# Layer 0's router gates, range count and weight means: one piece a tile, and a matmul three steps later

## The chip, the cores and the metric

The kernel runs on one core of a Trainium2 chip. The metric is device time in microseconds (us) of one launch. The engines are TensorE (PE; its weight loads are shown apart as PEld), VectorE (DVE), ScalarE (ACT), GpSimd (POOL), and SyncE (SP), which issues most DMAs here. Each engine works through its own queue of instructions; they meet at semaphores.

## The reference

Two layers of a metaformer on an image batch of 2 x 256 channels x 56 x 56. Each layer has a spatial mixer and a mixture of experts (MoE) over the 6272 pixels taken as tokens.

```python
# layer 0
x = x + window_attention(_ln_c(x))          # 7x7 windows, 8 heads of 32
t = tokens(x)
t = t + moe0(_ln_t(t))                      # 8 experts, top 2
# layer 1
x = x + ternary_conv_block(_ln_c(x))        # two 3x3 convolutions
t = tokens(x)
t = t + moe1(_ln_t(t))

def moe0(tokens):                           # D = 256, hidden 256
    probs = softmax(tokens @ router_w.T)
    rw, re = top_k(probs, 2);  rw = rw / max(rw.sum(-1), 1e-12)
    out = tokens
    for e in range(8):
        out = out + combine[:, e] * (gelu(tokens @ w1[e]) @ w2[e])

def ternary_weight(w):                      # of each of layer 1's two convolutions
    tw = w - mean(w)
    lo, hi = min(tw) + span / 3, max(tw) - span / 3
    return where(tw < lo, -1, where(tw > hi, 1, 0))
```

What the change touches is the gates of `moe0` (`rw` above), a check that no softmax sum left its range, and the `mean(w)` of the two ternary weights.

## The kernel before, in words

**Layer 0's attention** runs strip by strip (14 strips of 8 x 56 pixels). Each finished strip is normalised, routed and written, row by row of its chosen experts, into a DRAM table `xs` by indirect DMAs of POOL (L891). The largest logits and all logits are kept (`most`, `lgs`), so that the gates can be computed at once for all tokens by `gates0` (L906 to L925): DVE subtractions, two ACT exponentials (L915, L916), then DVE sums, reciprocals and products.

**Layer 0's experts** (`experts_in_order`, L1058) run over 56 tiles of 256 rows, each with one expert's weights. For each tile j the order of the instructions on SP, PE, ACT and DVE is written out by hand (`manual_schedule`):

- SP: `fetch_rows(j + 4)` (L1091) reads rows of `xs`; their place comes from a plan (`where`), a small table in SBUF that SP reads into a register. `fetch_weights(j + 3)` (L1102) reads 641 KB of expert weights.
- `turn(j + 2)`: PE transposes (L1112) into one PSUM buffer `pt`, ACT copies it out as `ut` (L1116), DVE computes destinations (L1119).
- `first(j + 1)`: 8 matmuls (L1144), two ACT gelus (L1151).
- `second(j)`: 8 matmuls (L1163) into one of two `py` buffers; DVE adds the bias into `y` (L1173). POOL scatters `y` into the DRAM table `ys` (L1175). The weight buffer (one of four) is free for `fetch_weights(j + 4)` after this DVE instruction.
- `beside(j)`: other work goes here, at the end of the tile, behind the tile's instructions in every queue.

Tiles 0 to 26 follow an early plan, made when 10 of the 14 strips were routed. The rest needs a second plan (`tiles0(1)`, L931 to L1045): a PE matmul that sums counts (L947), then some 30 small DVE instructions, up to `where` (L1036) and `held` (L1045).

`beside(j)` does the following. While late strips are still being routed, it advances them (`push`). Once none is left, which is in tile 21, it calls `routed_all`, all of it in that one tile: the second plan, the gates, the range count `unfit` on DVE (L1700 to L1703), the matmul `pf` that sums it over the partitions (L1705), and `flag` (L1706). Then it closes the attention's pools, opens the big buffer `x_all` and clears the convolution's borders with POOL memsets (L1722 to L1725). From the next tile on, `beside` takes four steps per tile of the generator `prepare`, which makes the two ternary weights.

**A ternary weight** (`ternary`, L1273) is loaded into `x_all` in pieces of 1024 columns (L1286) and goes through nine parts of 512 columns: DVE maximum (L1293) and minimum (L1295), ACT sum (L1298). Then DVE folds the parts (L1300, L1301), POOL takes the maximum over the partitions (`ext`, L1303), PE sums over the partitions with a matrix of ones (`psum_w`, L1305), and DVE computes the mean (L1307) and thresholds (from L1312, which reads `ext`). A second pass over the nine parts writes -1, 0 and 1 (L1329 to L1333), and last come the copies that the convolutions read (ACT L1340 for the second weight; L1345, L1346, L1826 and DVE L1352 for the first). A step ends at each `yield`: before, 53 steps for the first weight and 47 for the second.

**After the experts** layer 1 reads `ys` back strip by strip (L1215), adds, normalises, convolves, and runs its own MoE. The change leaves these stages as they are; they begin when the last rows of `ys` have landed.

Of the kernel before, what the change touches and what calls it, by code (L numbers as in the profile page):

```python
# [632 lines left out]
def metaformer(ctx: ExitStack, tc: tile.TileContext, a: dict, out: bass.AP, flag):  # L633
# [620 lines left out]
    def finish(steps):  # L1254

        while True:
            try:
                next(steps)
            except StopIteration as end:
                return end.value  # L1260
# [12 lines left out]
    def ternary(name, sums, ps_pool, tag, tp, at):  # L1273

        size = KC * TAPS * C
        wide = NTT * C  # L1280
        raw = x_all.rearrange("p s c -> p (s c)")[:, at * wide : at * wide + size]
        parts = [(n, raw[:, n : n + PART]) for n in range(0, size, PART)]

        def load(i):
            n = min(wide, size - i * wide)
            nc.sync.dma_start(raw[:, i * wide : i * wide + n], a[name + "_flat"][:, i * wide : i * wide + n])  # L1286

        st3 = tp.tile([P, 3, len(parts)], F32, tag="st3", name="st3")
        load(0)
        for i, (n, part) in enumerate(parts):  # L1290
            if n % wide == 0 and n + wide < size:
                load(n // wide + 1)
            nc.vector.tensor_reduce(st3[:, 0, i : i + 1], part, AX.X, ALU.max)  # L1293
            yield
            nc.vector.tensor_reduce(st3[:, 1, i : i + 1], part, AX.X, ALU.min, negate=True)  # L1295
            yield
            low = tp.tile([P, PART], F32, tag="low", name="low", bufs=1)
            nc.scalar.activation(low, part, AF.Copy, accum_out=st3[:, 2, i : i + 1])  # L1298
        st = tp.tile([P, 3], F32, tag="st", name="st")
        nc.vector.tensor_reduce(st[:, 0:2], st3[:, 0:2, :], AX.X, ALU.max)  # L1300
        nc.vector.tensor_reduce(st[:, 2:3], st3[:, 2, :], AX.X, ALU.add)  # L1301
        ext = tp.tile([P, 2], F32, tag="ext", name="ext")
        nc.gpsimd.partition_all_reduce(ext, st[:, 0:2], P, bass_isa.ReduceOp.max)  # L1303
        pt = ps_pool.tile([P, 1], F32, tag=tag, name="psum_w", bufs=3)
        nc.tensor.matmul(pt, ones, st[:, 2:3], start=True, stop=True)  # L1305
        mean = tp.tile([P, 1], F32, tag="w_mean", name="w_mean")
        nc.vector.tensor_scalar_mul(mean, pt, 1.0 / NW)  # L1307

        hi = tp.tile([P, 1], F32, tag="w_hi", name="w_hi")
        lo = tp.tile([P, 1], F32, tag="w_lo", name="w_lo")  # L1310
        third = tp.tile([P, 1], F32, tag="w_third", name="w_third")
        nc.vector.tensor_tensor(hi, ext[:, 0:1], mean, ALU.subtract)  # L1312
        nc.vector.scalar_tensor_tensor(
            lo, ext[:, 1:2], -1.0, mean, ALU.mult, ALU.subtract
        )
        span = tp.tile([P, 1], F32, tag="w_span", name="w_span")
        rest = tp.tile([P, 1], F32, tag="w_rest", name="w_rest")
        nc.vector.tensor_tensor(span, hi, lo, ALU.subtract)
        nc.vector.tensor_scalar_mul(third, span, 1.0 / 3.0)


        nc.vector.scalar_tensor_tensor(rest, third, -2.0, span, ALU.mult, ALU.add)
        nc.vector.tensor_tensor(rest, rest, third, ALU.subtract)
        nc.vector.scalar_tensor_tensor(third, rest, 1.0 / 3.0, third, ALU.mult, ALU.add)
        nc.vector.tensor_tensor(lo, lo, third, ALU.add)
        nc.vector.tensor_tensor(hi, hi, third, ALU.subtract)
        for n, part in parts:
            low = tp.tile([P, PART], F32, tag="low", name="low", bufs=1)
            nc.vector.tensor_scalar(low, part, mean, lo, ALU.subtract, ALU.is_lt)  # L1329
            yield  # L1330
            nc.vector.tensor_scalar(part, part, mean, hi, ALU.subtract, ALU.is_gt)
            yield
            nc.vector.tensor_tensor(part, part, low, ALU.subtract)  # L1333
            yield
        g = raw.rearrange("p (k y c) -> p k y c", k=KC, y=3)
        middle = g[:, :, 1, C : 2 * C]
        nc.vector.tensor_scalar_mul(middle, middle, 2.0)
        if sums.shape[2] == 3:
            for k in range(KC):
                nc.scalar.copy(sums[:, k], g[:, k])  # L1340
                yield
            return
        for k in range(KC):
            up, middle, down = (g[:, k, y, :] for y in range(3))
            nc.scalar.copy(sums[:, k, 0, :], up)  # L1345
            nc.scalar.copy(sums[:, k, 3, :], down)  # L1346
            nc.vector.tensor_tensor(up, up, down, ALU.add)
            yield
            nc.vector.tensor_scalar_mul(middle, middle, 0.5)
            yield  # L1350
            for c, op in ((1, ALU.add), (2, ALU.subtract)):
                nc.vector.scalar_tensor_tensor(sums[:, k, c, :], up, 0.5, middle, ALU.mult, op)  # L1352
                yield
# [4 lines left out]
    with ExitStack() as st:  # L1358
# [72 lines left out]
        norm0, settle0, tiles0, _, gates0, wgt0, counted0, sent0 = routing(0, aw, tp, ps)  # L1431
# [202 lines left out]
        plans0, taken = [], []  # L1634
# [54 lines left out]
        X, XT, pad, sums = {}, {}, {}, []  # L1689
# [4 lines left out]
        def routed_all():  # L1694

            nonlocal x_all
            plans0.append(tiles0(1, *taken))
            finish(gates0())
            unfit = aw.tile([TT, 1], F32, tag="unfit", name="unfit")
            nc.vector.tensor_scalar(fits, fits, float(len(STRIPS)), None, ALU.is_lt)  # L1700
            nc.vector.tensor_reduce(unfit, fits, AX.X, ALU.add)
            unfit_b = aw.tile([TT, 1], BF16, tag="unfit_b", name="unfit_b")
            nc.vector.tensor_copy(unfit_b, unfit)  # L1703
            pf = ps.tile([P, 1], F32, tag="aux", name="pf")
            nc.tensor.matmul(pf, all_w, unfit_b, start=True, stop=True)  # L1705
            nc.vector.tensor_scalar_min(flag, pf[0:1, :], 1.0)  # L1706
            st.close()

            xpool = mid_x.enter_context(tc.tile_pool(name="x", bufs=1, reuse_waits="tile"))


            x_all = xpool.tile([P, len(STRIPS), NTT * C], F32, tag="x", name="x")
            for i, (b, s) in enumerate(STRIPS):
                XT[b, s] = x_all[:, i].rearrange("p (t c) -> p t c", c=C)
                X[b, s] = x_all[:, i, : KC * NT].rearrange("p (k n) -> p k n", n=NT)

            for b in reversed(range(B)):
                cp = pads[b].enter_context(
                    tc.tile_pool(name=f"pads{b}", bufs=1, reuse_waits="tile")
                )  # L1720
                t = cp.tile([P, HC, KC, WC], F32, tag=f"pad{b}", name=f"pad{b}")
                nc.gpsimd.memset(t[:, 0:1], 0.0)  # L1722
                nc.gpsimd.memset(t[:, HC - 1 : HC], 0.0)
                nc.gpsimd.memset(t[:, 1 : HC - 1, :, 0:1], 0.0)
                nc.gpsimd.memset(t[:, 1 : HC - 1, :, WC - 1 : WC], 0.0)  # L1725
                pad[b] = t
            mid.enter_context(wq_held)
            wqp = wq_held.enter_context(tc.tile_pool(name="wq", bufs=1, reuse_waits="tile"))

            some = x_all[:, len(STRIPS) - 3 :].rearrange("p s c -> p (s c)").bitcast(BF16)  # L1730
            sums.append(some.rearrange("p (k n c) -> p k n c", k=KC, n=COMPS))
            sums.append(wqp.tile([P, KC, 3, 3 * C], BF16, tag="sums", name="sums"))

        def prepare():
            for i in range(2):
                yield from ternary(f"L1_conv_w{i + 1}", sums[i], ps0, "ph", tp0, 5 * i)

        steps = prepare()

        def beside(j):  # L1740
            push()
            if j == NTILE - 2:

                for i in range(X_FIRST):
                    nc.sync.dma_start(XT[STRIPS[i]][:TT], x_mid[i])
            if j == EARLY[0] - ROWS_AHEAD - 1:
                while under_way:
                    push()
            if len(plans0) > 1:
                for _ in range(4):  # L1750
                    next(steps, None)
            elif not under_way:
                routed_all()

        experts(0, C, plans0, ys[0], wp0, tp0, ps0, beside)
        for _ in steps:
            pass
        tiles_on.close()

    with mid:  # L1760
# [336 lines left out]
        with ExitStack() as both:  # L2097
# [50 lines left out]
            norm, settle, tiles, planning, gates, wgt1, _, sent = routing(1, wp, tp, ps)  # L2148
# [241 lines left out]
```

## Time and profile before

| | |
|---|---|
| Median of 3 runs | 1796.24 us (1790.43 to 1796.35) |
| The profiled execution's own time | 1794.06 us |
| Its span in the profile | 1792.3 us |
| Mean granted TensorE clock | 0.883 |
| PE busy | 1535.1 us (86%) |
| DVE busy | 970.1 us (54%) |
| ACT busy | 698.9 us (39%) |
| POOL busy | 672.7 us (38%) |

The profile is one execution. Times in it count from the start of its span. A group's idle time is that of its engine just before the instruction, with what ended it. A PE at 86% is not idle 14% evenly: the share is an average over stages that have different limits, so a change inside layer 0's experts is read from the stretch of some 200 us in which they run.

### The profile page before, as it was taken

The numbers are of one execution on the slowest core, as the hardware profiler recorded it, in microseconds if no ns is written. First come the engines' busy times: TensorE is split into PE (matmuls) and PEld (weight loads), VectorE is DVE, ScalarE is ACT, GpSimd is POOL, SyncE is SP. The second block draws the span as 40 slices with busy tenths as digits, with TensorE's granted clock in tenths as the row PEclk, the third lists the DMA queues.
The fourth block names the chain that finished last, engine by engine and source line by source line (L and its number), as shares of the span: only waits on it lengthen the run. The fifth ranks groups of instructions, "written<-read, shape, count | busy, mean of one in ns | idle before, by whom it ended". The sixth has DMA issues, their size and how long they took to land. (4 is left out here: it accounts for less than half of the span.)

```text
span 1792.3 us, 25968 instructions
## 1 busy us (share of the span) xinstructions
PE 1535.1 (86%) x8613; PEld 1202.6 (67%) x8613; DVE 970.1 (54%) x2697; ACT 698.9 (39%) x1358; POOL 672.7 (38%) x772
## 2 busy tenths in 40 slices
PE   5999998999878868894799979957579999999953
PEld 3555565556557747774688768846468888888842
DVE  4456666465635336864799888778633112111146
ACT  2544343443323324642444362234333334334312
POOL 2112445344343653543243323427715553222210
PEclk9999998999879888997799989955569999999975
DMA  7122334122266766976654000024447778888868
GB/s 233 41 64 85 107 92 131 58 75 62 77 192 213 246 205 226 321 250 201 175 155 126 8 0 1 11 62 128 125 159 268 267 244 287 288 289 286 288 178 287
DMA packets 91887, 291.78 MB, mean 163 GB/s; under 512 B 20487, under 2 KB 35803, under 8 KB 80416
## 3 DMA queue, kind: packets, MB, share of 16 engines
q1 hardware_dynamic: 66736, 231.79, 41.4%
q0 software_dynamic: 21200, 51.82, 8.1%
q10 hardware_dynamic: 3808, 6.42, 1.1%
q8 instruction: 70, 1.15, 0.3%
q14 instruction: 73, 0.60, 0.1%
HBM read 218.51 MB, written 74.20 MB: 163 GB/s over the span
## 5 line engine op out<-in xcount | busy, mean ns | idle before, releaser
L1144 PE MATMUL ph<-ut,w 128*128 128x256 f32 (+1 forms) x1472 | 315.1, 366 | 6.6 <-DMA w<-in_L_experts 6.5
L1173 DVE TENSOR_TENSOR y<-py,w 128x512 f32<-128x512 f32 (+1 forms) x120 | 76.8, 640 | 440.8 <-PE py L1163 362.3
L1163 PE MATMUL py<-w,h 128*128 128x256 f32 x1288 | 303.7, 384 | 7.1 <-issue 7.1
L1144 PEld LDWEIGHTS ph<-ut,w 128*128 128x128 f32 x1472 | 254.8, 197 | 36.0 <-DMA w<-in_L_experts 6.3
L1163 PEld LDWEIGHTS py<-w,h 128*128 128x128 f32 x1288 | 247.3, 194 | 42.5 <-issue 8.5
L891 POOL DMA_INDIRECT xs<-u,pos x224 | 219.0, 978 | 125.1 <-issue 53.6
L1175 POOL DMA_INDIRECT ys<-y,dest x136 | 137.1, 1008 | 246.3 <-DVE dest L1119 110.1
L1151 ACT ACTIVATE h<-ph,w 128x256 f32<-128x256 f32 (+1 forms) x368 | 162.9, 447 | 132.5 <-PE ph L1144 89.0
L1522 ACT ACTIVATE ex<-sc 112x476 f32<-112x476 f32 (+3 forms) x224 | 116.8, 572 | 176.3 <-PE sc L1512 165.4
L1116 ACT COPY ut<-pt 128x512 f32<-128x512 f32 (+1 forms) x120 | 65.2, 543 | 268.8 <-PE pt L1112 231.0
L1842 PE MATMUL pc<-lo,wq 128*128 128x448 f32 x336 | 132.2, 395 | 6.7 <-DVE lo L1817 6.6
L1842 PE MATMUL pc<-hi,wq 128*128 128x448 f32 x336 | 131.4, 393 | 2.2 <-DVE x L1866 2.0
L1532 PE MATMUL av<-ex,vals 112*64 112x238 f32 (+3 forms) x896 | 127.0, 406 | 5.3 <-DVE acc L1542 3.3
L1175 POOL DMA_INDIRECT ys<-y,to x81 | 82.3, 1016 | 130.9 <-DVE dest L1119 78.3
L1542 DVE TENSOR_TENSOR acc<-av,acc 128x238 f32<-128x238 f32 (+3 forms) x224 | 87.0, 406 | 75.1 <-PE av L1532 67.5
L1234 DVE SCALAR_TENSOR_TENSOR x<-got,wgt,x 112x256 f32<-112x256 f32 x216 | 102.6, 544 | 31.9 <-DMA got<-ys 31.5
L1985 PE MATMUL pc<-hi,wq 128*128 128x448 f32 (+1 forms) x288 | 103.4, 369 | 16.8 <-ACT hi L1952 9.4
L1503 PE MATMUL sc<-q_im,keys 32*112 32x238 f32 (+3 forms) x896 | 99.1, 424 | 7.1 <-ACT ex L1522 7.0
L1985 PE MATMUL pc<-lo,wq 128*128 128x448 f32 (+1 forms) x288 | 102.5, 365 | 0.2 <-DVE lo L1953 0.2
L1532 PEld LDWEIGHTS av<-ex,vals 112*64 112x64 f32 x896 | 57.1, 143 | 55.5 <-issue 27.7
L1815 POOL TENSOR_TENSOR v<-pad 128x928 f32<-128x928 f32 (+1 forms) x28 | 56.6, 2034 | 99.3 <-DVE lo L1817 49.1
L1112 PE MATMUL pt<-ident,xg 128*128 128x128 f32 x434 | 71.8, 287 | 15.9 <-DMA xg<-xs 9.5
(278 smaller groups left out, 2499.2 us busy)
## 6 DMA issues: line engine op xcount, KB each, us to landing
w<-in_L_experts SPq DMA_DIRECT2D x64, 1154.0 KB
w<-in_L_experts SPq DMA_DIRECT2D x56, 641.0 KB
xg<-xs SPq DMA_DIRECT2D x97, 260.0 KB
got<-ys SPq DMA_DIRECT2D x28, 896.0 KB
acc<-in_fresh SPq DMA_DIRECT2D x14, 896.0 KB
xt<-in_x_tok SPq DMA_DIRECT2D x14, 448.0 KB
xr<-in_x_tok SPq DMA_DIRECT2D x14, 448.0 KB
rec<-shares SPq DMA_DIRECT2D x28, 224.0 KB
```

Source lines behind the costliest of these rows:

```text
L891: w = nc.gpsimd.indirect_dma_start(xs[:, :], bass.IndirectOffsetOnAxis(ap=pos[:, j, t0 + t : t0 + t + 1], axis=0), us[t // NTT][:, t % NTT ...
L1144: nc.tensor.matmul(ph[:, :g], w1[:, k, f * P : (f + 1) * P], d["ut"][:, k, :g], start=k == 0, stop=k == KC - 1,)
L1151: nc.scalar.activation(d["h"][:, f, :g], ph[:, :g], AF.Gelu, bias=b1[:, f : f + 1])
L1163: nc.tensor.matmul(py[:, i, :], d["h"][:, f, i * P : (i + 1) * P], w2[:, f, :], start=f == 0, stop=f == NF - 1,)
L1175: o = nc.gpsimd.indirect_dma_start(ys[:, :], bass.IndirectOffsetOnAxis(ap=d["to"][:, i : i + 1], axis=0), y[:, i, :], None, bounds_check=T ...
L1234: nc.vector.scalar_tensor_tensor(xt[:, t, :], y[:, t, j, :], wgt[:, j, n : n + 1], xt[:, t, :], ALU.mult, ALU.add)
L1503: nc.tensor.matmul(sc[h // 2][:, h % 2, :nq], keys[g][p, c, tx * TT : (tx + 1) * TT], q_im[p, c, r0:r1, c0:c1], start=True, stop=False,)
L1522: nc.scalar.activation(e[:, :, :nq], sc[j][:, :, :nq], AF.Exp, scale=HD**-0.5)
L1532: nc.tensor.matmul(av[VW * i : VW * (i + 1), :nq], vals[g % 3][:, tx, 2 * c + j, 2 * i : 2 * i + 2, :].rearrange("p a d -> p (a d)"), ex[j ...
L1542: added = nc.vector.tensor_tensor(d, av[:, :nq].rearrange("p (h w) -> p h w", w=c1 - c0), d, ALU.add)
L1842: nc.tensor.matmul(pc[:, :NT], wq[:, k, c, dx * C + o * P : dx * C + (o + 1) * P], part[:, :, k, dx : dx + W], start=m == 0, stop=m == 2 * ...
L1985: nc.tensor.matmul(pc[:, : 2 * ns * W], wq[:, k, c, dx * C + o * P : dx * C + (o + 1) * P], part[:, : 2 * ns, k, dx : dx + W], start=m == ...
```

## The change

Three edits. In `ternary`, three `yield`s stand between POOL's `ext` and the matmul `psum_w`, so the matmul and everything after it comes three steps of the generator later; a weight has 56 and 50 steps. `routed_all` becomes a generator of four pieces: the plan; all of the gates; the count `unfit`; and the rest, from `pf` on. `beside` takes one piece a tile from tile 21 on, and begins with the steps of `prepare` once the last piece has filled `sums`.

```diff
@@ ternary
         ext = tp.tile([P, 2], F32, tag="ext", name="ext")
         nc.gpsimd.partition_all_reduce(ext, st[:, 0:2], P, bass_isa.ReduceOp.max)
+        for _ in range(3):
+            yield
         pt = ps_pool.tile([P, 1], F32, tag=tag, name="psum_w", bufs=3)
         nc.tensor.matmul(pt, ones, st[:, 2:3], start=True, stop=True)
@@ routed_all
             plans0.append(tiles0(1, *taken))
-            finish(gates0())
+            yield
+            for _ in gates0():
+                pass
+            yield
             unfit = aw.tile([TT, 1], F32, tag="unfit", name="unfit")
             nc.vector.tensor_scalar(fits, fits, float(len(STRIPS)), None, ALU.is_lt)
             nc.vector.tensor_reduce(unfit, fits, AX.X, ALU.add)
             unfit_b = aw.tile([TT, 1], BF16, tag="unfit_b", name="unfit_b")
             nc.vector.tensor_copy(unfit_b, unfit)
+            yield
             pf = ps.tile([P, 1], F32, tag="aux", name="pf")
             nc.tensor.matmul(pf, all_w, unfit_b, start=True, stop=True)
@@
         steps = prepare()
+        ends = routed_all()
 
         def beside(j):
@@
-            if len(plans0) > 1:
+            if sums:
                 for _ in range(4):
                     next(steps, None)
             elif not under_way:
-                routed_all()
+                next(ends, None)
```

## The prediction

> **What bounds the kernel now.** I read the slices first: PE is 90% busy or more nearly everywhere except around two changes of stage and a dip near 660 us. The chain that ended last is followed only back to 1174 us, so it says nothing of layer 0's experts; I use the waits of PE between 663 and 766 us, where all changed instructions lie:
>
> ```profile
> PE pf L1705 <- DVE unfit_b L1703: 12.6, 1, 12.6
> PE ph L1144 <- DMA w<-in_L_experts: 2.9, 2, 1.5
> PE psum_w L1305 <- issue: 2.9, 1, 2.9
> PE pt L1112 <- ACT ut L1116: 2.5, 1, 2.5
> PE psum_w L1305 <- DVE st L1301: 2.2, 1, 2.2
> ```
>
> The columns are total, times, longest. The reader is to see that the three matmuls which the change moves stop PE for 12.6, 2.9 and 2.2 us. PE's timeline shows what a stop costs (start, duration, instruction, idle time before):
>
> ```profile
> 656.10 0.59 PE L1163 MATMUL py<-w,h 128*128 128x256 f32 x2
> 659.32 2.93 PE L1163 MATMUL py<-w,h 128*128 128x256 f32 x6 [2.62 <-issue]
> 663.11 0.17 PE L947 MATMUL counts<-seen_all,all_w 112*128 112x8 bf16 x1 [0.86 <-DVE seen_all L945]
> 675.87 0.16 PE L1705 MATMUL pf<-unfit_b,all_w 112*128 112x1 bf16 x1 [12.60 <-DVE unfit_b L1703]
> 675.97 1.08 PE L1112 MATMUL pt<-ident,xg 128*128 128x128 f32 x4
> 676.85 3.19 PE L1144 MATMUL ph<-ut,w 128*128 128x256 f32 x8
> 679.88 1.89 PE L1163 MATMUL py<-w,h 128*128 128x256 f32 x8
> ...
> 695.45 1.89 PE L1163 MATMUL py<-w,h 128*128 128x256 f32 x8
> 699.58 0.38 PE L1305 MATMUL psum_w<-st,ones 128*128 128x1 f32 x2 [2.24 <-DVE st L1301]
> 699.83 1.00 PE L1112 MATMUL pt<-ident,xg 128*128 128x128 f32 x4
> 700.62 3.25 PE L1144 MATMUL ph<-ut,w 128*128 128x256 f32 x8
> ```
>
> An undisturbed tile takes 3.89 us from one start of L1163 to the next (691.55 to 695.45). After a stop, the next tile's transposes and first matmuls run at about half speed. From 695.45 to the next L1163 at 703.71 is 8.26 us, 4.37 too many: 2.24 idle, 0.25 for `psum_w`, 1.8 of slow clock. For the second weight it is 758.28 to 765.47, 3.30 too many, without slow clock. While PE stands before `pf`, DVE works through the plan, the gates and the count:
>
> ```profile
> 662.89 0.16 DVE L945 CAST seen_all<-seen 112x8 bf16<-112x8 f32 x1
> 671.05 0.22 DVE L1045 TENSOR_TENSOR held<-below,since 128x58 int32<-128x58 f32 x1
> 671.19 0.62 DVE L912 TENSOR_TENSOR lgs<-lgs,most 112x448 f32<-112x448 f32 x1
> 675.03 0.28 DVE L925 TENSOR_TENSOR wgt<-wgt,tot 112x112 f32<-112x112 f32 x1
> 675.66 0.16 DVE L1703 CAST unfit_b<-unfit 112x1 bf16<-112x1 f32 x1
> ```
>
> So 8.3 us of the stop is the plan, 4.1 the gates, 0.5 the count. The plan stays in one piece; it hurts PE only because `pf` stands ahead of tile 22 in PE's queue.
>
> **What the skill says.** TensorE: Matmul & The Clock Gate, "What's actually happening": the PE clock halves after an idle window of about 3.4 us and recovers after as long a busy one; the window runs free. The trace agrees in kind (8 matmuls in 3.19 to 3.25 us, not 1.89, after stops of 12.6 and 2.24 us; none slow after one of 2.85). The same page, "Architectural detail", calls ACT and DVE strict FIFOs; here `y` of tile 22 appears only after the gates and count. GPSIMD Engine Reference, "2.1 Instruction dispatch", gives about 6 us for the first call of newly loaded code; the first `ext` came 6.45 us after POOL was free (707.05), the second without such a wait.
>
> **The change, part by part.** No instruction is added but the generator's empty steps; the order of the built program moves `pf` behind tile 24 on PE, each `psum_w` behind one more tile, the two sets of weight loads three and four tiles later on SP, and `flag`'s register load on SP from before `fetch_weights(26)` to before the last weights, where one load of about 1.1 us (the gap between two SP issues) lies beside PE's work. POOL keeps the first border's memsets where they were, with the same waits; the other border's go between scatters of tiles 23 and 24, 1 us in all, hidden because POOL needs 2.6 of 3.9 us a tile.
>
> *A, the plan's stop.* (A tile j is here the stretch that ends with second(j); its transposes are for j + 2.) Now tile 22 starts on PE at 663.3, its rows and weights issued by 653.8. By the rows above:
> - Tile 22: transposes at 0.9, first 2.8 (half slow), second 1.7: ends at 668.7.
> - Tile 23: 3.9, ends at 672.6. It needs no DVE result: `py` has two buffers.
> - DVE ends the plan at 671.3, then destination and `y(22)` (0.2 and 0.6) to 672.2, gates 4.1 to 676.3, `y(23)` to 677.2, count 0.5.
> - ACT, in the written order, stands at the exponential until L912 is done (672.8), needs 0.9 for both, then copies `ut(25)` by 674.6, reloads gelu's table (1.28) and gives its first gelu at 676.4. This is the new stop: with one `pt` buffer, tile 24's transposes wait from 672.6 to 674.7, and its second hidden block waits for a `ph` buffer until 676.5. Tile 24 ends at 679.2.
> - SP: `where` exists at 670.8, rows of `xs` at 670.0 (POOL's memset saw them), so `fetch_rows(27)` goes at 672, weights 26 at 673.1, weights 27 after `y(23)` at 677.4. A weight load takes 3.9 to 5.6 us under load (issued 711.37 and 715.29, used 715.30 and 720.89): landed by 681.3 to 683, wanted at 683.6.
>
> Before, tile 24 ended at 689.4. The gain is 10.2; less 1.2 for a likely slow clock after the 2 us stop: **9.0**, bounds 5 and 11.5.
>
> *B, the sums.* `st` is ready 2.2 to 2.8 us after the tile's second matmuls, the moved matmul comes 3.9 after: no wait. It keeps 0.25 to 0.4 us of its own. Gains 4.0 and 3.0: **7.0**, bounds 4 and 7.5. What doesn't go: for the first weight `ext` still comes some 10 us after that tile, so DVE still stands before L1312, now 5 us instead of 7.3, with the next tile's `y` behind it. In both orders that `y` ends some 13.9 us after the tile at which `st` is made, its weights go out then, and the two stops of 1.5 and 1.4 us for `w` remain.
>
> *C, the last copies.* With three steps more per weight, the second weight's L1337 is the first step of tile 51 instead of the third of tile 46. ACT's two copies of 2.1 us start 1.2 us earlier in their tile, and PE's stop of 3.08 us before 797.69 shrinks: **1.2**, bounds 0 and 3. Work ends four tiles ahead of tile 55, so nothing spills behind the experts.
>
> *D, the first weight's loads.* Before, they were issued at 675.76, before PE moved, and needed by ACT at 680.85. Now SP issues them behind tile 28's weights, while ACT asks for them about 1.4 us later (686.89 and 688.24 in a later tile). Landing took 7.1 us for the second weight (738.23 to 745.34), and ACT held `ut` back. ACT can be some 4.7 us late before PE notices (L1298 at 688.24, next transposes at 693.07, less 0.8). With half such a landing cost exposed: **-1.5**, bounds 0 and -3.8 (the whole loss of the tile at 746.58: 7.66 less 3.89).
>
> Sum: 9.0 + 7.0 + 1.2 - 1.5 = **15.7 us** off. What follows waits for the last scatter, and that for PE's last tile (828.1; scatter 831.24, read back 833.49), so it carries through. Against the profiled execution's 1794.06 that gives 1778.4; its time is 2.2 below the median of the runs, against which I state 1796.2 - 15.7 = **1780.5**.
>
> **The rivals.**
> 1. *The wait moves to ACT.* If exponential, table and late `y` hold PE for two tiles with slow clock each time, A falls to 5, B to 4 (clock phases), C stays 1.2 and D costs 3.8: 6.4 off, 1790. For it: ACT's strict order. Against: four weight buffers and two `py`.
> 2. *Slower: POOL's code load.* It took 6.45 us with DMA at a share of 0.31 (700 to 710), because SP stood behind DVE. Now PE keeps going and DMA is nearer the 0.90 of 710 to 760. If the load is stretched, DVE stands before L1312, `y` and the weights behind it, and PE loses it one for one, since it already stops for `w` there. Against the 15.7 gained it decides from about 16 us of stretch, and makes 1806 with 25. Against: queues are separate, and `w` loads stretched only from 3.9 to 5.6.
> 3. *It does nothing*: if stops in the dense DMA window merely move (PE, ACT and DVE stood together near 640 and 658 for reasons not named here), net gain about 2: 1794.
>
> **How the numbers follow.** No change within about 0.5% (9 us) can be told from none. Forecast 0.78; rival 1 0.10; rival 3 0.05; rival 2 0.07. The two middle ones land within 0.5%, and a little of the forecast's low tail too, against some larger gains of rival 1: faster 0.78, same 0.15, slower 0.07. The bounds of A to D added give 5 to 22 off; with rival 1 and 3 inside, the range is 1773 to 1794.
>
> **What would show it.** Right: tile 22's L1112 within 1 us of L947; no PE wait on `unfit_b` or `st`; PE idle 1 to 3 us before tile 24's L1112, released by ACT `ut`; DVE before L1312 waiting about 5 us; last L1163 near 809 instead of 824.5. Wrong: a PE wait for `w` over 3 us before tile 30, or POOL's first `ext` more than 8 us after its release.

## The result, and the profile after

The changed kernel takes 1774.97 us (median of 9 runs, 1769.49 to 1787.94) against 1795.11 us for the kernel before (9 runs, 1781.28 to 1805.59). The ratio is 0.9899, 95% interval 0.9869 to 0.9929: about 20 us less, and the interval lies below 1. The profiled execution took 1779.46 us, with a span of 1777.7 us and a mean granted clock of 0.887.

Waits of PE from 668 to 780 us (total, times, longest):

```profile
PE pt L1112 <- ACT ut L1116: 6.4, 3, 2.5
PE ph L1144 <- DMA w<-in_L_experts: 2.8, 3, 1.7
PE counts L947 <- DVE seen_all L945: 0.9, 1, 0.9
PE py L1163 <- DVE y L1173: 0.7, 1, 0.7
```

The waits for `unfit_b` and `st` are gone. What is left comes from ACT's copy `ut`, three times, and from the expert weights. PE's timeline shows where the stops now lie:

```profile
671.22 0.17 PE L947 MATMUL counts<-seen_all,all_w 112*128 112x8 bf16 x1 [0.86 <-DVE seen_all L945]
671.32 0.63 PE L1112 MATMUL pt<-ident,xg 128*128 128x128 f32 x4
...
682.01 0.66 PE L1112 MATMUL pt<-ident,xg 128*128 128x128 f32 x4 [2.18 <-ACT ut L1116]
...
684.77 1.89 PE L1163 MATMUL py<-w,h 128*128 128x256 f32 x8
686.50 0.17 PE L1711 MATMUL pf<-unfit_b,all_w 112*128 112x1 bf16 x1
...
692.92 1.89 PE L1163 MATMUL py<-w,h 128*128 128x256 f32 x8
697.36 0.66 PE L1112 MATMUL pt<-ident,xg 128*128 128x128 f32 x4 [2.55 <-ACT ut L1116]
697.86 3.14 PE L1144 MATMUL ph<-ut,w 128*128 128x256 f32 x8
700.79 2.38 PE L1163 MATMUL py<-w,h 128*128 128x256 f32 x8
...
714.68 0.28 PE L1307 MATMUL psum_w<-st,ones 128*128 128x1 f32 x2
...
725.64 1.99 PE L1163 MATMUL py<-w,h 128*128 128x256 f32 x8 [0.67 <-DVE y L1173]
729.74 1.99 PE L1144 MATMUL ph<-ut,w 128*128 128x256 f32 x8 [1.66 <-DMA w<-in_L_experts]
734.70 1.99 PE L1144 MATMUL ph<-ut,w 128*128 128x256 f32 x8 [0.81 <-DMA w<-in_L_experts]
809.86 0.66 PE L1112 MATMUL pt<-ident,xg 128*128 128x128 f32 x4 [1.87 <-ACT ut L1116]
```

(Behind the edits the changed kernel's line numbers are 2 to 6 higher: `pf` is L1711, `psum_w` L1307, and the thresholds begin at L1314.) `pf` and `psum_w` now pass without a wait. The stop of 12.60 us has shrunk to 2.18, two tiles later. New is the stop at 697.36, followed by matmuls at a slow clock.

To compare runs I use one stretch, **T**: from the start of L947 to the start of second(55), the last eight L1163. Where the trace prints tiles 54 and 55 as one row of 16, its start plus 1.89 us is taken (0.16 more than the start of its ninth matmul, alike before and after). **S** in the first expectations ends at the start of that row, so there T is S plus 1.89. T was 163.3 us before and 146.2 after: 17.1 less. The rest of the span doesn't explain the gain: up to L947 the run was 8.1 us longer (663.1, then 671.2), behind T it was 5.6 shorter. These two belong to what stays open.

| part of T, tiles and time over an undisturbed tile | before | after | gain | predicted |
|---|---|---|---|---|
| A, from L947 to the start of second(24) | 24.55 | 13.55 | 11.0 | 9.0 |
| B, the two tiles with `psum_w` (8.26 and 7.19, now 4.07 each) | 15.45 | 8.14 | 7.3 | 7.0 |
| the stops for `w` behind `ext` (tiles 30, 31; now 33 to 35) | 3.45 | 3.95 | -0.5 | 0 |
| C, the second weight's last copies (tiles 48, 49; now 53) | 5.0 | 2.1 | 2.9 | 1.2 |
| D, the first weight's first loads (tiles 27, 28) | none | 4.5 | -4.5 | -1.5 |
| the second weight's first loads (tiles 37, 38; now 41, 43, 44) | 4.4 | 3.2 | 1.2 | 0 |

They add up to 17.4; the other tiles differ by 0.3 in sum.

### The profile page after: what moved, and what is told of

It is laid out like the page before. It is cut to its first block, busy times and chain, and to the rows that moved or that the text cites. A ratio compares the mean times of both kernels' runs of the same rounds, so it can differ in the third digit from the quotient of the medians.

```text
span 1777.7 us, 25965 instructions
## 1 busy us (share of the span) xinstructions
PE 1530.2 (86%) x8613; PEld 1198.8 (67%) x8613; DVE 971.0 (55%) x2697; ACT 697.7 (39%) x1358; POOL 672.3 (38%) x772
## 5 line engine op out<-in xcount | busy, mean ns | idle before, releaser
L1144 PE MATMUL ph<-ut,w 128*128 128x256 f32 (+1 forms) x1472 | 312.2, 363 | 8.7 <-DMA w<-in_L_experts 5.8
L1163 PE MATMUL py<-w,h 128*128 128x256 f32 x1288 | 299.8, 381 | 1.1 <-DVE y L1173 0.7
L1144 PEld LDWEIGHTS ph<-ut,w 128*128 128x128 f32 x1472 | 252.0, 196 | 38.9 <-DMA w<-in_L_experts 6.3
L1163 PEld LDWEIGHTS py<-w,h 128*128 128x128 f32 x1288 | 244.4, 191 | 35.4 <-issue 1.3
```

The source lines that it names most:

```text
L1144: nc.tensor.matmul(ph[:, :g], w1[:, k, f * P : (f + 1) * P], d["ut"][:, k, :g], start=k == 0, stop=k == KC - 1,)
L1163: nc.tensor.matmul(py[:, i, :], d["h"][:, f, i * P : (i + 1) * P], w2[:, f, :], start=f == 0, stop=f == NF - 1,)
```

## The experiments

The kernels ran in three groups, each group on one chip with runs of the kernel before beside it; the table is in their order, four to a group. T is of one profiled execution each; most executions of one kernel lie within some 14 to 25 us in time, so a T alone is trusted only where its tiles show the place.

| run | L947 at | T | time, median | ratio to before (95%) |
|---|---|---|---|---|
| before, again | 632.2 | 169.3 | 1764.44 | |
| changed, again | 639.1 | 152.4 | one run, 1746.66 | |
| split alone | 639.6 | 167.6 | 1754.36 | 0.9918 (0.9888 to 0.9948) |
| wait alone | 631.1 | 154.3 | 1744.94 | 0.9907 (0.9870 to 0.9943) |
| changed, third | 672.0 | 149.5 | one run, 1792.68 (before: 1805.74) | |
| loads early | 675.9 | 144.2 | 1780.75 | 0.9830 (0.9781 to 0.9879) |
| seven steps | 673.0 | 142.4 | 1783.47 | 0.9879 (0.9820 to 0.9938) |
| rows first | 685.4 | 144.7 | 1793.31 | 0.9926 (0.9893 to 0.9958) |
| changed, timed | 668.6 | 148.3 | 1779.05 (before: 1795.89) | 0.9921 (0.9886 to 0.9956) |
| loads early and seven steps | 661.3 | 144.3 | 1769.52 | 0.9862 (0.9816 to 0.9908) |
| the same, plan in one piece | 663.2 | 150.3 | 1778.99 | 0.9909 (0.9883 to 0.9936) |
| product alone | 673.7 | 150.7 | 1783.25 | 0.9916 (0.9894 to 0.9938) |

### The two kernels again

No edit.

> The kernel before, profiled once more. The measure for all runs is the stretch S from the start of the plan's matmul L947 to the start of the last L1163 of layer 0's experts: 161.4 us before, 144.3 after. Theory (the change acts inside S alone): S is 161.4 within 1.5 us again, with PE stopped about 12.6 us before pf and 2 to 3 us before each psum_w, while the time up to L947 (663.1) and the time from S's end to the end of the span (967.8) scatter by several us. Rival (the edit also moves what stands before and behind S): both parts repeat within 1 us.

> The changed kernel, profiled once more. Theory: S is 144.3 within 1.5 us; the 671.2 us up to L947 and the 962.2 us behind S do not repeat better than several us, and overlap those of the kernel before. Rival: the part before L947 is again some 8 us longer than in the kernel before and the part behind S some 5.6 us shorter, as in the first pair of profiles; then these belong to the change.

Both missed the size of S (167.4 and 150.5 us). Their difference, 16.9, is close to the 17.1 of the first pair, but it is made up differently. Up to the start of second(25) the change gained 10.6 us in the first pair and only 2.6 here; behind it, it gained 6.5 and 14.2. In this pair the stops at `psum_w` before the change had cost 11.3 us (4.8 and 6.4), not 7.7, and the last copies 6.3, not 5.0. So the sum repeats and its parts do not. The changed kernel again came 7 us later to L947 (639.1 against 632.2), as the rival of the second had it, while behind S it was only 1.2 us shorter (955.2 against 956.4). The reason for the 2.6 is a stop that the changed kernel didn't have in the first pair. Its timelines of PE, POOL and SP:

```profile
655.91 0.17 PE L1711 MATMUL pf<-unfit_b,all_w 112*128 112x1 bf16 x1
659.55 0.63 PE L1112 MATMUL pt<-ident,xg 128*128 128x128 f32 x4 [3.48 <-DMA xg<-xs]
662.79 3.78 PE L1144 MATMUL ph<-ut,w 128*128 128x256 f32 x8 [2.60 <-DMA w<-in_L_experts]
```

```profile
654.27 0.94 POOL L891 DMA_INDIRECT xs<-u,pos  x1 [0.30 <-issue]
657.14 0.20 POOL L1728 MEMSET pad<- 128x116 f32 x1 [1.93 <-DMA xs<-u,pos]
```

```profile
639.05 0.34 SPq L1102 DMA_DIRECT2D w<-in_L_experts  x1
656.87 0.35 SPq L1091 DMA_DIRECT2D xg<-xs  x1
```

SP stands from 639 to 656.87, when POOL's last write of `xs` (issued at 654.27) has landed; then it reads tile 27's rows, and only behind them the next weights. POOL has been alternating two writes of `xs` and two of `ys`, 1.28 us apart, for tiles. L947 was 15.2 us ahead of the last write of `xs` here, and 2.7 us ahead in the first pair. So where PE is early against POOL, the plan's stop turns into a stop for rows.

### One part at a time

Split alone: the `yield`s ahead of `psum_w` are taken out.

```diff
         nc.gpsimd.partition_all_reduce(ext, st[:, 0:2], P, bass_isa.ReduceOp.max)
-        for _ in range(3):
-            yield
         pt = ps_pool.tile([P, 1], F32, tag=tag, name="psum_w", bufs=3)
```

> Only routed_all in pieces; psum_w waits no steps. Theory, by parts read from the first pair of traces: the plan's stop gives 11.0 back (PE starts tile 22 within 0.3 us of L947, one stop of about 2 us before tile 24's transposes), the late loads of the first weight cost 4.5, psum_w stops PE 2 to 3 us twice as before: S 155 (153 to 157). Rival, most of the gain is that of the sums: S above 159. Rival, the loads' loss comes from the wait of three steps: S about 150.

Wait alone: `routed_all` as before, the `yield`s kept.

```diff
-            yield
-            for _ in gates0():
-                pass
-            yield
+            finish(gates0())
...
-            yield
             pf = ps.tile([P, 1], F32, tag="aux", name="pf")
```

> Only the three steps between ext and psum_w; routed_all stays whole. Theory: PE stops 12.6 us before pf as before; both psum_w waits vanish (4.2 and 3.1 with the slow clock), the stop at the second weight's last copies shrinks (2.9), the two stops for w behind ext stay near 3 to 4 in sum, no loss by late first loads: S 151 (149 to 153.5). Rival, the psum_w waits come back as a wait of DVE for ext that reaches PE: S 156 to 159.

The wait alone hit: S 152.4, no wait at `psum_w`, and the stop of 12.6 us before `pf` still there. The split alone missed: S 165.8, where its rival (most of the gain is that of the sums) had said over 159. Its `psum_w` stops stayed at 2.91 and 2.84 us, so B belongs to the wait; its tiles 24 and 25 took 8.66 and 13.30 us:

```profile
660.04 0.63 PE L1112 MATMUL pt<-ident,xg 128*128 128x128 f32 x4 [3.46 <-DMA xg<-xs]
664.13 3.78 PE L1144 MATMUL ph<-ut,w 128*128 128x256 f32 x8 [3.46 <-DMA w<-in_L_experts]
```

In this stretch most of what A won at tile 22 was lost at tile 25. Against the kernel before in this group (169.3) T fell by 1.7 us with the split alone, by 15.0 with the wait alone and by 16.9 with both: here nearly all of the gain in T is the wait's. By time the split alone is still 0.9918, and the two ratios multiplied (0.983) promise more than both together gave (0.990 and 0.992). The profiled execution of the split alone (span 1763.0) lies above its median, that of the kernel before (1756.0) below its own, so how much the split is worth in time in this group stays open; in T it is worth less than where rows are in time, which the wait for `xg` shows.

### The late loads, DVE's wait, the rows

> The changed kernel again, as the base for the three kernels beside it; no part is left out. S is the time from the start of the second plan's matmul of counts (L947) to the start of layer 0's last L1163. In the two runs so far S was 144.3 us (no wait of PE for rows of xs) and 150.5 us (PE waited 3.48 us for xg at tile 25, and 2.6 us for w behind it). Theory (rows limit): S is near 144 if the last indirect write of xs is issued less than 5 us behind L947, as in the first of the two (2.7 us), and near 150 if more than 12 us behind, as in the second (15.2 us). Rival (chance): S lies anywhere from 143 to 152 without regard to that distance.

S was 147.6 with the last write of `xs` 2.8 us behind L947: near neither of the two values, so this distance isn't the only thing that sets S. No wait for `xg`.

Loads early: both first loads come ahead of four empty steps.

```diff
         load(0)
+        load(1)
+        for _ in range(4):
+            yield
...
-            if n % wide == 0 and n + wide < size:
+            if n and n % wide == 0 and n + wide < size:
```

> The changed kernel, but each ternary weight's first two loads are issued four empty steps (one tile) ahead of the first part that reads them. Theory (term D: what the changed kernel loses where the first weight begins is the landing of loads that are issued too late): the waits of ACT L1298 and DVE for x at the first weight's first part, 4.25 and 3.94 us in the first run of the changed kernel, go below 1 us, PE's stop before the transposes behind it (2.55 us) goes, and the second weight's first tile (41: 1.94 over an undisturbed one) loses most of its excess. S is 3 to 6 us shorter than that of the changed kernel beside it, if that shows the loss at tile 27; 1.5 to 3 us shorter if it doesn't. Rival (the DMA queues are full there, so that an earlier load only displaces an expert weight): the waits for x go, a PE wait for w of 2 us or more stands in their place, S within 1.5 us of the changed kernel's.

The last tiles print apart here, so its figure is T: 144.2 against 149.5, 5.3 us shorter, inside the 3 to 6 of the theory. The loss stood where it said: tiles 27 and 28 were 4.6 us too long in the changed kernel beside it, here 1.1 in sum. The second weight's first tiles went from 3.9 us too many (tiles 41 to 45) to 1.7 (43 and 47), while the tiles behind `ext` went from 5.9 to 7.2. PE where the stop was:

```profile
699.43 1.89 PE L1144 MATMUL ph<-ut,w 128*128 128x256 f32 x8
701.16 1.89 PE L1163 MATMUL py<-w,h 128*128 128x256 f32 x8
703.00 0.63 PE L1112 MATMUL pt<-ident,xg 128*128 128x128 f32 x4
704.33 1.99 PE L1144 MATMUL ph<-ut,w 128*128 128x256 f32 x8 [0.70 <-DMA w<-in_L_experts]
```

One part of the expectation failed: ACT still waits for `x`, up to 2.2 us at a time, but PE no longer notices. At these tiles the rival's wait for `w` is 0.70 us, not 2.

Seven steps: `range(7)` in place of `range(3)` ahead of `psum_w`.

> The changed kernel, but seven empty steps instead of three ahead of psum_w, so that DVE reaches the thresholds (the first reader of ext) one tile later. Theory: PE's stops for w at tiles 33 to 35 (0.84 + 2.04 + 1.07 us over undisturbed tiles in the first run of the changed kernel) come from DVE standing 5.4 us for ext with the tile's y behind it, which holds back the next expert weight; with four steps more DVE waits under 2 us there, the three tiles lose 3 us or more of their excess, and S is 2.5 to 4.5 us shorter than that of the changed kernel beside it. Rival (the stops come from the transfers alone: weights of x and of the experts share the DMA engines): DVE's wait goes but the stops for w stay, S within 1.5 us. POOL's first ext comes 6 to 7 us after its release in either case.

T was 142.4 against 149.5, more than the 2.5 to 4.5 expected. The tiles give the part that is the edit's: the excess behind `ext` fell from 5.9 us (tiles 33 to 35) to 2.2 (35 and 36), 3.7 us; most of the rest lies at tiles 27, 28 and 41 to 47, where the loads begin, which the edit only shifts or doesn't touch. DVE's wait, first in the changed kernel beside it, then here:

```profile
DVE w_hi L1314 <- POOL ext L1303: 7.2, 1, 7.2
```

```profile
DVE w_hi L1314 <- POOL ext L1303: 3.2, 1, 3.2
```

So most of the loss behind `ext` is DVE's wait, with `y` behind it; transfers alone would have kept it. What remains there (2.2 us) this run doesn't explain. Two details of the expectation failed: DVE still waits 3.2 us, not under 2, and `ext` came 8.0 us after POOL was free, not 6 to 7.

Rows first: POOL's writes of `ys` are held back two tiles up to tile 21.

```diff
-            for i in range(gp):
-                o = nc.gpsimd.indirect_dma_start(
+            held_back.append((gp, d["to"], y))
+            while len(held_back) > (2 if not layer and j < 22 else 0):
+                gp, to, y = held_back.pop(0)
+                for i in range(gp):
+                    o = nc.gpsimd.indirect_dma_start(
...
```

> The changed kernel, but POOL's two indirect writes of ys of a tile are issued two tiles later up to tile 21, and all that are held back go out at tile 22; so the last writes of xs stand ahead of up to four writes of ys (1.28 us each). Nothing is left out. Theory (rows limit: where PE reaches tile 25 early it waits for the rows of the second plan, which SP reads once the last write of xs has landed): the last write of xs is issued about 5 us earlier against L947 than in the changed kernel beside it. If that one waits for xg at tile 25, the wait goes and S is 4 to 8 us shorter; if not, S is the same within 1.5 us. Rival (POOL isn't what orders the rows; the plan or SP is): the wait for xg stays within 1 us of what it was.

Inconclusive. The changed kernel beside it had no wait for `xg` to take away. The last write of `xs` came 5.3 us ahead of L947 instead of 2.8 behind, but because L947 itself came at 685.4, after PE had stood 10.25 us for DVE's `seen_all`. Stops of 4.4 to 10.1 us stand there in four other kernels without this edit, so they can't be laid to it. S was 142.8, 4.8 us shorter, where the theory without such a wait said the same within 1.5; 2.2 us of that lie behind `ext`, which came 5.8 us after POOL was free here and 7.9 beside it. The time, 0.9926, is no gain over the changed kernel.

### Both together, and the split taken apart

> The changed kernel once more, timed, as the base of the three kernels beside it; nothing is left out. From here the stage is measured from the start of L947 to the start of second(55), the last eight L1163 (called T): 146.2, 152.4 and 149.5 us in the three profiled runs of the changed kernel, 163.3 and 169.3 in those of the kernel before. Theory: T is 146 to 153 again, and the ratio to the kernel before 0.990, between 0.986 and 0.994. Rival (the change's worth depends on the chip by more than that): a ratio outside.

T 148.3, ratio 0.9921: as expected. Here PE lost more behind `ext` than in the first pair; POOL and PE:

```profile
719.87 0.37 POOL L1303 PARTITION_ALL_REDUCE ext<-st  x1 [8.79 <-issue]
```

```profile
724.84 3.29 PE L1163 MATMUL py<-w,h 128*128 128x256 f32 x8 [3.21 <-DVE y L1173]
727.93 1.02 PE L1112 MATMUL pt<-ident,xg 128*128 128x128 f32 x4
```

Loads early and seven steps: the two edits above, and five steps a tile from tile 44 on.

```diff
-                for _ in range(4):
+                for _ in range(4 if j < 44 else 5):
                     next(steps, None)
```

> The changed kernel with the loads one tile ahead and seven empty steps instead of three; from tile 44 on five steps of the generator a tile instead of four, so that it still ends beside the experts. Theory (the two losses are separate: late loads at tiles 27, 28 and 41, DVE's wait for ext at tiles 33 to 35): T is 7 to 11 us shorter than the changed kernel's beside it, near 140, and the time some 8 us shorter. Rival (both gains come from the same transfers, and what was seen with one alone, 5.3 and 7.1 us, doesn't add): T only 4 to 7 us shorter, with PE waits for w of 3 us or more in sum between tiles 28 and 40.

From tile 25 to 49 the excess over undisturbed tiles fell from 13.3 to 5.3 us: 8.0, in the range for the two together. But T fell by only 4.0, the low end of what the rival had said (its 3 us of waits for `w` were 2.4), because the last copies, which come eight steps later per weight (four for the loads, four ahead of `psum_w`), met the last tiles. ACT and PE there:

```profile
797.69 2.11 ACT L1345 CAST sums<-x 128x2304 bf16<-128x2304 f32 x1 [7.76 <-DVE x L1342]
799.71 0.58 ACT L1116 COPY ut<-pt 128x512 f32<-128x512 f32 x1
```

```profile
800.34 3.50 PE L1144 MATMUL ph<-ut,w 128*128 128x256 f32 x8 [5.30 <-ACT sums L1345]
```

ACT waited 7.76 us for DVE's L1342 (L1337 in the kernel before), the step behind its last pass, with `ut` behind it, PE 5.30 us and then ran slow: tile 54 took 10.53 us, some 7 too many, where the changed kernel lost 2.1 at tile 53. The time is 9.5 us less than the changed kernel's (1769.52 and 1779.05); the intervals of the two ratios overlap, so this is the lowest median of its group and no more.

The same steps ahead of `psum_w` and the same early loads, with plan, gates and count in one piece as before (so the weights begin three tiles sooner, and four steps a tile are kept to the end). Against the changed kernel, the loads' edit left out:

```diff
-            yield
-            for _ in gates0():
-                pass
-            yield
+            finish(gates0())
...
         nc.gpsimd.partition_all_reduce(ext, st[:, 0:2], P, bass_isa.ReduceOp.max)
-        for _ in range(3):
+        for _ in range(7):
             yield
```

> As the kernel before in its second plan, gates and count (all in tile 21, pf ahead of tile 22), but with the loads one tile ahead and seven empty steps ahead of psum_w. Theory: PE stops for 12 to 13 us before pf, and T is 148 to 152 (154.3 with three steps alone, less 4 for the loads and DVE's wait). The profiled kernels in which the plan isn't split reached L947 7 to 8 us sooner on both chips; if that belongs to the split, this kernel's L947 comes 6 us or more ahead of the other's with the same loads and steps, and their times lie within 4 us of each other. Rival (it is no property of the split: each kernel falls differently there, as the 522 to 542 us at which the first L1163 of the experts came in ten profiled runs suggest): L947 isn't 6 us ahead, and this kernel's time is 7 us or more over the other's.

T was 150.3 (the last row's first matmuls ran slow, so the start of its ninth is taken), as expected, with the stop before `pf`:

```profile
675.99 0.16 PE L1710 MATMUL pf<-unfit_b,all_w 112*128 112x1 bf16 x1 [12.65 <-DVE unfit_b L1708]
```

From L947 to the start of second(24) it took 24.6 us, with the split 13.5; the kernel with the split gave back some 3 us of this at its last tiles. L947 came at 663.2, not ahead of the 661.3 of the kernel with the split, and the time was 9.5 us over: as the rival had it. That the split has no part in coming late doesn't follow, though; see what stays open.

Product alone: plan, gates and count in tile 21, only `pf` and what follows three tiles later.

```diff
-            yield
-            for _ in gates0():
-                pass
-            yield
+            finish(gates0())
...
-            yield
+            for _ in range(3):
+                yield
             pf = ps.tile([P, 1], F32, tag="aux", name="pf")
```

> The changed kernel, but the plan, all gates and the count stay together in tile 21, and only pf, flag and what follows come three tiles later, as in the changed kernel; the three steps ahead of psum_w stay. Theory of the prediction (the plan's stop came from pf's place in PE's queue alone, and gates in a tile of their own bring nothing but a sooner y(22)): T is within 3 us of the changed kernel's beside it, with one PE stop of 2 to 5 us at tile 23 or 24, released by ACT, and none for unfit_b. Rival (gates ahead of y(22) in DVE's queue hold back y, py and the expert weights, so that most of the stop comes back): PE stops of 6 us or more in sum between L947 and tile 26, T 5 us or more longer.

T was 150.7, 2.4 over the changed kernel's. PE had one stop at tile 23, released by ACT:

```profile
673.72 0.17 PE L947 MATMUL counts<-seen_all,all_w 112*128 112x8 bf16 x1 [10.07 <-DVE seen_all L945]
674.71 3.35 PE L1144 MATMUL ph<-ut,w 128*128 128x256 f32 x8
...
683.81 0.66 PE L1112 MATMUL pt<-ident,xg 128*128 128x128 f32 x4 [4.03 <-ACT ut L1116]
684.31 3.46 PE L1144 MATMUL ph<-ut,w 128*128 128x256 f32 x8
```

From L947 to the start of second(24) it took 17.9 us, in the changed kernel beside it 14.7, and in the kernel with the plan in one piece 24.6. Some 1.9 us of the 17.9 are slow matmuls of tile 22 (the eight L1144 took 3.35 us) behind the stop of 10.07 us ahead of L947, which the changed kernel beside it didn't have. So most of A, about 7 to 9 of 10 us, is `pf`'s place in PE's queue. Gates in a tile of their own are worth little: T differs by 2.4 us, of which about one is the longer stop (4.03 us, where the changed kernel beside it had 3.00).

## Why the prediction was right, and where its sum was not

The forecast (1780.5, range 1773 to 1794, faster) held: 1775.0 in the first comparison, 1779.1 in the last against the same level of before (1795.9). Its 15.7 us stand against 20.1 and 16.8 by medians, and 17.1 in T, where all its terms lie. That the sum came so near is in part luck: A, B, C and the second weight's first loads gave 5.2 us more than said, D, the stops for `w` and the other tiles 3.8 less. The next pair had nearly the same T gain from other parts, with A almost spent on the rows.

**A, 9.0 said, 11.0 measured.** The mechanism was as told, step by step. ACT in the profile after:

```profile
680.73 0.58 ACT L915 ACTIVATE lgs<-lgs 112x448 f32<-112x448 f32 x1 [2.13 <-DVE lgs L912]
681.21 0.28 ACT L916 ACTIVATE wgt<-wgt 112x112 f32<-112x112 f32 x1
681.39 0.57 ACT L1116 COPY ut<-pt 128x512 f32<-128x512 f32 x1
```

ACT stands at the exponential, the copy `ut` behind it, and PE starts the transposes at 682.01, 10.8 us after L947 (the working had 11.6). The stop is 2.18 us, as the 2 said. The step that failed is "less 1.2 for a likely slow clock after the 2 us stop": the matmuls behind it ran at full speed (two times four L1144 in 1.03 and 1.13 us). In other runs of the changed kernel the matmuls behind it did run slow (stops of 3.00 and 3.12 us, tile 24 at 8.55 and 8.90). What the working took as given, rows of `xs` by 670, is true only where PE isn't ahead of POOL; in the first group SP read them 17.8 us after L947, not 7, and cost tile 25 more than 8 us. That bound wasn't in the range of A.

**B, 7.0 said, 7.3 measured** (10.9 in the pair of the first group), and no wait at `psum_w` in any kernel that keeps the `yield`s. The stops for `w` remained as said (3.45 us of excess before, 3.95 after), as did DVE's stand before L1314 (L1312 in the prediction's numbering):

```profile
721.06 0.16 DVE L1314 TENSOR_TENSOR w_hi<-ext,w_mean 128x1 f32<-128x1 f32 x1 [5.43 <-POOL ext L1303]
```

**C, 1.2 said, 2.9 measured,** inside its bounds of 0 to 3. The stop shrank from 3.08 to 1.87 us as said; unsaid was that the slow clock behind it would go too. Before, with 1.89 us for the same eight L1144 after:

```profile
797.69 0.66 PE L1112 MATMUL pt<-ident,xg 128*128 128x128 f32 x4 [3.08 <-ACT ut L1116]
798.18 2.87 PE L1144 MATMUL ph<-ut,w 128*128 128x256 f32 x8
```

**D, -1.5 said, -4.5 measured,** outside its bound of -3.8: the term that was mis-sized. SP issues the loads, ACT waits for them:

```profile
690.58 0.33 SPq L1286 DMA_DIRECT2D x<-in_L_conv_w_flat  x2
```

```profile
696.12 0.63 ACT L1298 ACTIVATE low<-x 128x512 f32<-128x512 f32 x1 [4.25 <-DMA x<-in_L_conv_w_flat]
696.74 0.57 ACT L1116 COPY ut<-pt 128x512 f32<-128x512 f32 x1
```

The landing took 5.5 us, less than the 7.1 that the working feared. The failed step is "ACT can be some 4.7 us late before PE notices". ACT asks at 691.87, needs 1.24 us from L1298 to PE's next transposes (696.12 to 697.36), and PE was done at 694.81 (697.36 less 2.55): a slack of 1.7 us, not 4.7. The working's own figures don't give 4.7 either: 693.07 less 688.24 less 0.8 is 4.0, and these transposes start at 693.28 in the timeline before. They come from one tile of before, in which ACT started L1298 5.0 us ahead of PE's next transposes, where here it asked 2.9 us before PE was done. Then came 1.7 us of slow clock (3.14 and 2.38 us where 1.89 each is full speed; the granted clock was 0.50 from 699.3 to 701.3 us), which the term left out. In five other profiles with `pf` moved and the loads not moved ahead, tiles 27 and 28 lost 1.9 to 4.6 us; in the first group, where PE had just stopped at tile 25, they lost nothing.

**Rival 1** (the wait moves to ACT) is in the profile, once and for 2.18 us: the place was right and the size was the forecast's. **Rival 3** is refuted by A and B. **Rival 2** (POOL's code load stretched) was not seen in the first pair, where `ext` came 6.45 us after its release as before. Later it was, in small. In the four profiles of the changed kernel POOL's time for `ext` and PE's stop for `y` behind it go together: 6.45 and 0.67 us, 6.37 and 0.63, 7.92 and 2.40, 8.79 and 3.21. A stretch of 2.3 us cost PE 2.5: one for one, as that rival said, but of a size far from the 16 us at which it would decide. GPSIMD Engine Reference, "2.1 Instruction dispatch", of the Trainium skill has about 6 us for such a first call; over fourteen profiles it was 5.79 to 8.79 us here.

**What stays open.** The profiled kernels reach L947 at 631 to 685 us, and the first L1163 of the experts starts at 522 to 542, though the edits leave the order of instructions up to there as it was, but for the held writes of rows first. In the first pair and the first group the split kernels came to L947 7 to 8.5 us later than the others; in the last group one came 1.9 us sooner than the kernel in one piece, the other two 5.4 and 10.5 later. The first L1163 sorts them more plainly: 522.2 to 527.6 us in the four profiles in which the plan isn't split, 528.8 to 542.2 in the ten others. So the split may cost time ahead of L947 that T doesn't count; each is one execution, on different chips, and no trace here names a cause. The first pair's 8.1 us lost ahead of L947 and 5.6 won behind T can't be laid to a part of the change; the trace names `seen_all`, which stands behind DVE's `y`, as what PE mostly waits for at L947 (0.9 to 10.25 us), not why that differs. How much of the 20 us in time is the split's and how much the wait's is open too: each alone gave about what both gave.

## What to carry to other kernels

A small matmul that waits for a long chain of another engine costs the whole chain if it stands ahead of a pipeline's next tile; move that matmul behind the work that doesn't need it, and count what the old stop had hidden: here the loads of a weight that went out before PE started again, and the rows that POOL was still writing. Read slack at the place where the moved step will stand, from the asking engine to the next instruction of the bound engine, not from a tile of the old order. When two pieces of side work share a fixed number of steps ahead of a deadline, empty steps put into one push the end of the other toward the deadline: here the second weight's last copies met the last tiles.

## What the runs showed that I had not expected

- A stop of PE well under 3.4 us can be followed by slow matmuls. Between L947 and the last tile of all fourteen profiles, each of the 22 stops of 3.00 us or more was (over 0.30 us from one start to the next in the first matmuls behind it, where full speed has 0.22). Of the shorter ones some were (2.24, 2.51, 2.55 and 2.69 us) and some were not (2.18, 2.56, 2.85 and 2.94); 2.71 was in one profile and not in another. TensorE: Matmul & The Clock Gate, "What's actually happening", of the Trainium skill has an idle window of about 3.4 us that runs free; stops below it halved the clock here, so a stop of 2.2 to 3 us has to be priced with and without some 1.7 us of slow clock.
- POOL's last write of `xs` went out from 15.5 us behind L947 to 3.9 us ahead of it in kernels whose code up to there is the same. What the plan's stop hides depends on it.
- Each part of the change alone gave a ratio near that of both (0.9918, 0.9907, and 0.9899 to 0.9921 together), and in T of one group the wait alone gave 15.0 of 16.9 us.
